# A masked attention and graph convolution kernel: the adjacency and the mask allocated ahead of the small constants

## The chip, the cores and the metric

The kernel runs on one core of one Trainium2 chip. The metric is device time in microseconds (us) of one execution; less is better. TensorE is called PE, its weight loads PEld, VectorE DVE, ScalarE ACT, GpSimd POOL, and SyncE SP.

## The reference

Two layers are applied to `x` of 32 batches x 512 nodes x 512 features, with one 512 x 512 adjacency of zeros and ones for all batches. The first is attention with 8 heads of 64 features, in which only neighbours count. The second is a graph convolution with the adjacency normalized by degrees. Each adds its input and ends in a layer norm.

```python
# layer 0
q, k, v = (x @ W + b, as 8 heads of 64)        # Wq, Wk, Wv: 512 x 512
scores = einsum('bihd,bjhd->bhij', q, k) / sqrt(64)
scores = scores + where(adj == 0, -1e9, 0)
x = layernorm(x + einsum('bhij,bjhd->bihd', softmax(scores), v))
# layer 1
d = rsqrt(adj.sum(axis=1))                     # 0 where the degree is 0
norm_adj = adj * d[:, None] * d[None, :]
x = layernorm(x + einsum('nm,bmo->bno', norm_adj, x @ weight) + bias)
```

## The kernel before

All the work is in `unshifted` (line 50). `general` (line 1006) is a fallback for numbers out of range, which a test at the end starts only where it is needed.

**Memory.** Tiles come from pools. `consts` (line 87) holds what lives through the whole kernel; its tiles lie one behind the other in the order in which the program asks for them, each rounded up to 32 bytes per partition. `acts`, `work` and `small` lie behind it. A tile of 128 partitions has the same offset in each of them. The pool `consts` begins with the large tiles `xT`, `wv`, `wk`, `wq`, `w1` and the bias rows; then, from line 240 on, come `ident`, `minus_half`, `half`, `sel`, `spread`, `FINE`, and then `maskT`, `adjT` and `dis`. `FINE` takes 160 bytes, two and a half times 64. In the built program `maskT` begins at byte 93,856 and `adjT` at byte 95,904 of each partition; both leave 32 when divided by 64. All other large tiles leave 0.

**What the two tiles hold.** `adjacency(m)` (line 264) transposes a block of 128 columns of the adjacency on PE, and makes two tiles of it: `maskT`, one byte per element (255 where there is no edge), and `adjT`, the transposed adjacency, 4 blocks of 512 elements of 4 bytes in the type fp32r. All other matmul operands but the two that go with it are plain fp32. This happens once, in the first batch.

**Who reads them.** `scores` (line 402) reads `maskT` on DVE: one instruction of 1024 elements for each pair of heads and block of keys, which takes the scores out of PSUM and subtracts the mask; ACT then takes the exponential. `convolve` (line 666) reads `adjT` as the moving operand of its matmuls. The degree scaling is in the other operand: `norm` and `low` write the scaled input as two fp32r tiles, `HI` (its rounded value) and `LO` (what is left), and `first(d)` adds up both products:

```python
for m in range(NT):
    tensor.matmul(p, HI[b][:, m, ts(d, P)], adjT[:, m, :], start=m == 0, stop=False)
    tensor.matmul(p, LO[b][m][:, ts(d, P)], adjT[:, m, :], start=False, stop=m == NT - 1)
take(d, p, scalar.copy)
```

With 4 values of d, 4 of m and 2 parts that makes 32 matmuls of 128 x 128 weights on 128 x 512 moving elements in each of the first 31 batches. The last batch runs the same 32 in another order, in `block(m)`, as soon as each part is there. `compare(m)` reads `adjT` on DVE four times in the first batch.

**The other matmuls.** All 512 x 512 products with weights (`keys_and_queries`, `values_of`, and `second` in `convolve`) go through `seven` or a like list of 7 pieces in the place of 8 (sums and differences of halves of the operands are made beforehand on DVE and POOL). Each piece is of matmuls with 256 moving columns into one PSUM bank. `scores` and `values` are the attention's two products, with 512 moving columns and 64 rows or columns of the array each.

**The order.** Every engine's instructions stay in the order in which the program issues them (`InOrder`, line 34), and this order is written out by hand in the loop over blocks of one batch and two heads (from line 864). A batch's convolution stands among the attention of the next one, as a list of pieces. After `first` come the combinations of zT on POOL (`parts`), the rest of a set of keys and queries for the batch after on PE, and then `second`. Of PSUM's eight banks, three pairs (`WIDE`, line 95) go round among scores and pieces, one more bank takes every fourth piece, and one holds the product with the values.

Of the kernel before, what the change touches and what calls it, by code (L numbers as in the profile page):

```python
# [11 lines left out]
U8 = mybir.dt.uint8  # L12
F32R = mybir.dt.float32r
# [4 lines left out]
P = 128  # L18
# [31 lines left out]
def unshifted(  # L50
# [29 lines left out]
    B, N, D = x.shape  # L80
    NT = N // P
# [5 lines left out]
    consts = ctx.enter_context(tc.tile_pool(name="consts", bufs=1))  # L87
# [27 lines left out]
    def load_x(b, j):  # L115


        if b == 1 and j == 1:
            X[b, j] = work.tile([P, 8, DT, 32], F32, name="x1", tag="e", bufs=6)
        else:  # L120
            X[b, j] = acts.tile([P, 8, DT, 32], F32, name="x", bufs=1)
        for q in range(4):
            nc.sync.dma_start(
                X[b, j][32 * q : 32 * (q + 1)],
                x[b, ts(j, HALF), ts(q, P)].rearrange("(k s) (t r) -> s k t r", s=32, r=32),
            )
# [109 lines left out]
    if B > 1:  # L236
        load_x(1, 0)
        load_x(1, 1)

    ident = consts.tile([P, P], F32, name="ident")  # L240
    make_identity(nc, ident)
    minus_half = consts.tile([P, NT], F32, name="minus_half")
# [12 lines left out]


    FINE = consts.tile([P, B + 2 * NT], F32, name="fine")
    maskT = consts.tile([P, NT, N], U8, name="maskT")
    adjT = consts.tile([P, NT, N], F32R, name="adjT")
    dis = consts.tile([P, NT], F32, name="dis")  # L260

    plainT = acts.tile([P, NT, N], F32, name="plainT", tag="hi", bufs=1)
# [977 lines left out]
def kernel(tc: tile.TileContext, *args: bass.AP):  # L1240


    bad = unshifted(tc, *args)
    with tc.If(bad > 0):
        general(tc, *args)
# [39 lines left out]
```

## Time and profile before

| | us |
|---|---|
| median of three runs | 2773.66 (2773.32 to 2774.48) |
| span of the profiled execution, first to last instruction | 2771.4 |
| PE busy | 2748.6 |
| DVE busy | 2237.2 |
| POOL busy | 1786.7 |
| ACT busy | 1053.9 |
| matmuls with adjT and HI, 496 in 31 batches | 201.7 |
| matmuls with adjT and LO, 496 in 31 batches | 196.0 |

The profile is of one execution, and its page gives that execution's span and no other time of its own; the median of the runs is 2.3 us above the span. Nearly every line of the page says L44, the line of the helper through which all instructions pass, so a group is known by its tiles: `mm<-adjT,hi` is a matmul into a bank `mm` that reads `adjT` and `hi`. Of a matmul the page gives the latency. Matmuls are pipelined, so what one takes of PE's time is the distance from its start to the start of the next, which the timeline gives. A plain fp32 matmul stands in the trace as two records, and one with fp32r operands as one.

### The profile page before, as it was taken

To read this page: it belongs to the slowest core of one execution; us is meant where nothing else is said; L and a number is where in the kernel's file an instruction comes from. 1 tells how busy PE (TensorE), PEld (TensorE's weight loads), DVE (VectorE), ACT (ScalarE), POOL (GpSimd) and SP (SyncE) were. 2 spreads that over 40 slices of the span, in tenths; PEclk is the share of its full clock that TensorE was granted. 3 is DMA by queue.
4 is the path that set the end of the run, shared out by engine and by line. 5 is a ranking of instruction groups with operands and counts; after the bars stand their busy time and mean duration, and the time that the engine had idled before them with its cause. 6 is when DMAs were issued, how large, how long until landed. Compare 5 with 4: busy or idle time off the path is not lost. (4 is left out here: it accounts for less than half of the span.)

```text
span 2771.4 us, 34559 instructions
## 1 busy us (share of the span) xinstructions
PE 2748.6 (99%) x12540; PEld 1882.6 (68%) x12540; DVE 2237.2 (81%) x3199; ACT 1053.9 (38%) x1324; POOL 1786.7 (64%) x1171
## 2 busy tenths in 40 slices
PE   9999999999999999999999999999999999999997
PEld 7667676676776766766767667676676676766755
DVE  6878888778877788878887878887778887888787
ACT  2234333434334343343433343433434334343343
POOL 3666567666676666766666766667666676666666
PEclk9999999999999999999999999999999999999999
DMA  4111112111121111211112211112111121111211
GB/s 122 35 39 40 51 55 51 50 45 46 54 61 43 51 45 48 60 46 54 39 51 56 49 52 46 46 54 62 43 50 46 47 60 46 54 39 51 64 35 51
DMA packets 379108, 141.05 MB, mean 51 GB/s; under 512 B 277808, under 2 KB 345392, under 8 KB 378928
## 3 DMA queue, kind: packets, MB, share of 16 engines
q1 hardware_dynamic: 377776, 137.17, 19.2%
q8 instruction: 101, 1.65, 0.3%
q10 hardware_dynamic: 1152, 1.57, 0.2%
q14 instruction: 79, 0.65, 0.1%
HBM read 71.83 MB, written 33.55 MB: 38 GB/s over the span
## 5 line engine op out<-in xcount | busy, mean ns | idle before, releaser
L44 ACT ACTIVATE e<-e 128x1024 f32<-128x1024 f32 x512 | 540.8, 1057 | 718.9 <-DVE e L44 699.9
L44 DVE SCALAR_TENSOR_TENSOR e<-sc,maskT 128x1024 f32<-128x1024 f32 x512 | 605.3, 1214 | 62.9 <-PE av L44 42.1
L44 POOL TENSOR_TENSOR acc<-acc,e 128x1024 f32<-128x1024 f32 x248 | 589.1, 2375 | 89.7 <-ACT e L44 77.5
L44 POOL TENSOR_TENSOR acc<-e 128x1024 f32<-128x1024 f32 x126 | 298.8, 2372 | 331.6 <-ACT e L44 331.4
L44 PE MATMUL sc<-kq 64*128 64x512 f32 x2048 | 476.7, 603 | 0.4 <-DVE e L44 0.4
L44 PE MATMUL av<-e,v 128*64 128x512 f32 x2048 | 467.9, 598 | 0.0
L44 PE MATMUL mm<-xT,wk 128*128 128x256 f32 x1792 | 463.3, 381 | 0.0
L44 PE MATMUL mm<-xT,wq 128*128 128x256 f32 x1792 | 459.9, 379 | 0.0
L44 PE MATMUL mm<-wv,xT 128*128 128x256 f32 x1792 | 401.4, 381 | 1.7 <-issue 1.2
L44 PEld LDWEIGHTS mm<-xT,wk 128*128 128x128 f32 x1792 | 337.3, 190 | 72.3 <-DVE e L44 26.0
L44 PEld LDWEIGHTS mm<-wv,xT 128*128 128x128 f32 x1792 | 335.4, 190 | 72.3 <-DVE e L44 24.3
L44 PEld LDWEIGHTS mm<-xT,wq 128*128 128x128 f32 x1792 | 340.5, 190 | 46.3
L44 PEld LDWEIGHTS sc<-kq 64*128 64x128 f32 x2048 | 183.6, 186 | 258.3 <-DVE e L44 118.3
L44 PEld LDWEIGHTS av<-e,v 128*64 128x64 f32 x2048 | 135.4, 136 | 316.3 <-issue 269.9
L44 POOL TENSOR_TENSOR yT<-yT,xr 128x512 f32<-128x512 f32 x124 | 153.7, 1270 | 149.2 <-DVE yT L44 149.2
L44 POOL TENSOR_TENSOR yT<-yT,b_r 128x512 f32<-128x512 f32 x124 | 157.3, 1304 | 140.2 <-DVE lo L44 140.2
L44 PE MATMUL mm<-w,zT 128*128 128x256 f32 x992 | 224.6, 379 | 0.0
L44 DVE TENSOR_TENSOR e<-e,mm 128x512 f32<-128x512 f32 x224 | 152.9, 683 | 82.9 <-PE mm L44 82.7
L44 ACT ACTIVATE y<-y,add,rstd 128x512 f32<-128x512 f32 x127 | 96.2, 805 | 317.3 <-POOL add L44 317.3
L44 PEld LDWEIGHTS mm<-w,zT 128*128 128x128 f32 x992 | 188.2, 190 | 27.0 <-DVE wq L44 0.8
L44 PE MATMUL mm<-adjT,hi 128*128 128x512 f32 x496 | 201.7, 407 | 0.0
L44 PE MATMUL mm<-adjT,lo 128*128 128x512 f32 x496 | 196.0, 395 | 0.0
(144 smaller groups left out, 3211.9 us busy)
## 6 DMA issues: line engine op xcount, KB each, us to landing
out_dram<-y SPq DMA_DIRECT2D x127, 256.0 KB, 2.1
x<-in_x_dram SPq DMA_DIRECT2D x248, 128.0 KB, 2.7
yT<-yb SPq DMA_DIRECT2D x496, 64.0 KB, 2.4
xr<-in_x_dram SPq DMA_DIRECT2D x122, 256.0 KB, 3.4
wk<-in_L_gnn_Wk_dram SPq DMA_DIRECT2D x8, 128.0 KB, 4.9
wq<-in_L_gnn_Wq_dram SPq DMA_DIRECT2D x8, 128.0 KB, 4.4
yT<-in_adj_dram SPq DMA_DIRECT2D x1, 1024.0 KB, 5.9
w<-in_L_gnn_weight_dram SPq DMA_DIRECT2D x2, 512.0 KB, 7.4
```

The lines of the kernel that those rows point to most:

```text
L44: return self.tc.keep_in_program_order(op(*args, **kwargs))
```

## The change

The two tiles are asked for before the small constants and no longer after them, with `adjT` first. Nothing else in the program is changed.

```diff
         load_x(1, 0)
         load_x(1, 1)
 
+    adjT = consts.tile([P, NT, N], F32R, name="adjT")
+    maskT = consts.tile([P, NT, N], U8, name="maskT")
     ident = consts.tile([P, P], F32, name="ident")
     make_identity(nc, ident)
     minus_half = consts.tile([P, NT], F32, name="minus_half")
...
     FINE = consts.tile([P, B + 2 * NT], F32, name="fine")
-    maskT = consts.tile([P, NT, N], U8, name="maskT")
-    adjT = consts.tile([P, NT, N], F32R, name="adjT")
     dis = consts.tile([P, NT], F32, name="dis")
```

In the built program `adjT` then begins at byte 92,352 and `maskT` at byte 100,544 of each partition, both multiples of 64. The six small tiles move up by 10,240 bytes, which is 160 times 64. `dis` and everything behind it keep their places, and each engine has the same instructions in the same order.

## The prediction

> **What bounds the kernel now.** I read the page's first two parts first, to see which engine sets the end.
>
> ```profile
> PE 2748.6 (99%) x12540; PEld 1882.6 (68%) x12540; DVE 2237.2 (81%) x3199; ACT 1053.9 (38%) x1324; POOL 1786.7 (64%) x1171
> ...
> PEclk9999999999999999999999999999999999999999
> ```
>
> TensorE is busy in 99% of the span at the full granted clock. A busy PE could still be a waiting PE, so the view of waits, limited to PE, comes second:
>
> ```profile
> PE mm L44 <- DMA xr<-in_x_dram: 4.6, 1, 4.6
> PE sc L44 <- DVE lo L44: 1.5, 1, 1.5
> PE mm L44 <- issue: 1.2, 1, 1.2
> ```
>
> These are its three longest; all of them together come to under 10 us in 2771 (the rest of PE's idle time lies before its first and behind its last matmul). PE waits for nobody in the loop, so what a matmul costs is what the kernel costs. Which matmuls cost more than they must? The third view is the list of groups with shapes kept apart (the last two numbers before the second bar are busy us and mean ns of one):
>
> ```profile
> L44 PE MATMUL mm<-xT,wq 128*128 128x256 f32 x1792 | 459.9, 379 | 0.0
> ...
> L44 PE MATMUL mm<-w,zT 128*128 128x256 f32 x992 | 224.6, 379 | 0.0
> ...
> L44 PE MATMUL mm<-adjT,hi 128*128 128x512 f32 x496 | 201.7, 407 | 0.0
> L44 PE MATMUL mm<-adjT,lo 128*128 128x512 f32 x496 | 196.0, 395 | 0.0
> ```
>
> A mean here is a latency, since matmuls overlap; the cost on PE is the distance from start to start. The timeline of PE in one batch gives it (start, length, then the instruction):
>
> ```profile
> 1030.16 0.59 PE L44 MATMUL mm<-adjT,hi 128*128 128x512 f32 x1
> 1030.59 0.40 PE L44 MATMUL mm<-adjT,lo 128*128 128x512 f32 x1
> 1030.82 0.39 PE L44 MATMUL mm<-adjT,hi 128*128 128x512 f32 x1
> 1031.05 0.40 PE L44 MATMUL mm<-adjT,lo 128*128 128x512 f32 x1
> ...
> 1037.59 0.39 PE L44 MATMUL mm<-adjT,lo 128*128 128x512 f32 x1
> 1037.82 1.03 PE L44 MATMUL mm<-xT,wk 128*128 128x256 f32 x4
> 1038.68 1.03 PE L44 MATMUL mm<-xT,wq 128*128 128x256 f32 x4
> 1039.55 1.03 PE L44 MATMUL mm<-xT,wk 128*128 128x256 f32 x4
> 1040.41 1.03 PE L44 MATMUL mm<-xT,wq 128*128 128x256 f32 x4
> 1041.27 1.03 PE L44 MATMUL mm<-w,zT 128*128 128x256 f32 x4
> ```
>
> From 1030.59 to 1037.82 stand 31 matmuls of adjT: 7.23 / 31 = 233.2 ns each. From 1037.82 to 1041.27 stand 16 records of plain fp32: 3.45 / 16 = 215.6 ns each. The same difference, 395 - 379 = 16 ns, is in the two mean latencies above.
>
> **How the two kinds compare.** keys_and_queries issues 2 x 7 x 2 x 2 = 56 matmuls a batch, 1792 in 32 batches; the page has 1792 records with wk and 1792 with wq, so a plain fp32 matmul is two records. convolve's first() issues 32 a batch, 992 in 31 batches, and the page has 496 + 496: an adjT matmul is one record. Two records for 256 fp32 columns take 431 ns, one record for 512 fp32r columns takes 233 ns. So per column a record of adjT takes 233.2 / 512 = 0.46 ns, and one of plain fp32 215.6 / 256 = 0.84 ns: the adjacency is streamed 1.85 times as fast as any other of the large moving operands. If reading the moving operand can ever be short, it is here.
>
> **What the Trainium skill says.** (1) "TensorE: Matmul & The Clock Gate", section "Back-to-back issue gap", gives N/2.4 + 2.5 ns between starts with a warm clock, 215.8 ns for N = 512. The 216 ns of the fp32 records agree if each is two passes of 256; adjT's 233 is 17.4 above it. (2) "FP8 and Floating Point Precision", "TensorE Precision Notes": true fp32 takes four passes, the reduced form reads 4-byte values and truncates them. Two records of two passes each, against one record, agree. (3) "SBUF — State Buffer", "A bandwidth-pool intuition that's wrong (but worth ruling out)", puts the moving operand's path at about 614 GB/s. adjT's matmuls read 128 x 2048 bytes in 233.2 ns, 1124 GB/s, so the trace disagrees with that as a ceiling and the measurement decides. (4) The same page's "Operand start alignment" is about what is legal, "not speed". So no page prices a start at 32 modulo 64; the estimate has to come from the trace.
>
> **The change part by part.** The instruction streams of the two programs are the same on all five engines; only addresses move. In the built program adjT begins at byte 95,904 of a partition (32 modulo 64) and goes to 92,352 (0 modulo 64). maskT goes from 93,856 (32) to 100,544 (0). ident, minus_half, half, sel, spread and FINE move up by 10,240 bytes, 160 x 64, and keep their remainder. dis and all that follows stay where they were. All other large moving operands (xT, wv, w1, kq, e, zT, parts) are at 0 modulo 64 already.
>
> - adjT as moving operand: the one item with a price. The trace shows no fp32r matmul with an aligned start, so I bound it. Best: the 215.8 ns that an array bound by its columns needs, 17.4 ns less than now. Zero: the 17.4 ns belong to streaming 4-byte elements at this rate, wherever they start. A loss isn't excluded (third rival). I take the best, because the excess appears exactly in the only operand that is both misaligned and streamed at the full rate. Its size hardly depends on the slice m, the output block or hi against lo (231 to 235 ns at most positions), which is what a property of the whole tile gives.
> - Sum: 31 batches x 32 x 17.4 ns = 17.3 us. The first matmul of a batch takes 430 ns rather than 233, on top of the columns, and should keep that extra. In the last batch the first 16 of the 32 matmuls stand among waits for lo and hi (2733.9 to 2739.8); the last 16 are back to back, 16 x 17.4 = 0.3 us. Together 17.6 us.
> - maskT: read by 512 DVE instructions of 1214 ns on 1024 elements, some 1.19 ns per element, the same as the transposes of 1236 that read no mask. Cost nothing either way; and DVE, at 81%, would hide it.
> - adjT's writes (four ACT casts of 586 ns, beside four ACT copies to plainT, already at 0 modulo 64, of 592 ns) and the four compares on DVE: nothing.
> - The moved small constants: same instructions, same remainders, nothing.
>
> **Does it reach the end?** A batch's adjT block would end 32 x 17.4 = 0.56 us sooner. What is late next is POOL's chain of zT differences, which second() needs:
>
> ```profile
> 1040.27 1.28 POOL L44 TENSOR_TENSOR parts<-zT 128x512 f32<-128x512 f32 x1
> 1041.63 1.27 POOL L44 TENSOR_TENSOR parts<-zT,parts 128x512 f32<-128x512 f32 x1
> ```
>
> POOL works on other things right before it, so it would not start sooner. The second result is there at 1042.90; PE takes it up at 1044.72, after two pieces that don't need it. That cover is 1.8 us, and 1.3 us are left with PE 0.56 sooner. DVE waits 1.6 us for PE's next piece at 1039.75, so it has room too, and being in step with PE in every batch neither debt adds up. I let all of it through: span 2771.4 - 17.6 = 2753.8. The page gives the profiled execution no time but its span; the median of the runs, 2773.66, lies 2.3 us above it, and I carry that over: 2756.1 us, 0.63% less.
>
> **Rivals.**
> 1. Nothing happens: the 17.4 ns are the price of streaming fp32r. For it: no other operand goes at this rate, so speed and alignment can't be told apart in this trace. Against it: the excess isn't a neat share of the 512 columns (8%). 2773.7 us.
> 2. Part of it: the read goes in pieces of 64 bytes, 33 of them with a start at 32 and 32 without, and the rate is short all the same. An estimate from the trace: (233.2 - 2.5) / 33 = 7.0 ns a piece, one piece less on 1008 matmuls: 7.1 us, 2766.6 us. A gain half eaten by a late POOL or DVE would end in the same region.
> 3. Slower: the weights of the next matmul (hi, lo, both at 0 modulo 64) are loaded during the running one. With adjT in the same phase their reads could hold each other up. At one 64-byte piece of adjT, 7.2 ns, for each of the 8 pieces of a 512-byte weight row, 58 ns on 1008 matmuls: +58 us, 2832 us. It decides from one such collision a matmul (over 5.5 ns, 5.6 us) if nothing is gained. Against it: plain fp32 loads weights under aligned operands with no trace of it, though at the lower rate.
>
> **How the numbers follow.** Full gain 0.65, part 0.12, nothing 0.15, slower 0.08. A measurement of this kernel can tell about 0.2%, 5.5 us, from no change; the part case (7.1 us) is beyond that. So faster 0.77, same 0.15, slower 0.08. The full gain alone reaches from 2753 (the 2.5 ns go as well, 1008 x 2.5 = 2.5 us) to 2759. With part it holds 0.77, too little, so the range reaches to no change: 2753 to 2775.
>
> **What would show it.** Right: the 31 adjT matmuls from the second on in 6.69 us rather than 7.23, latencies near 379, every other PE distance as before, PE's waits still under 10 us. Rival 1: 233 again. Rival 2: some 226. Rival 3: over 235, or longer weight loads than 188 ns. Wrong in the last step: 216 ns but new PE waits for POOL parts or DVE.

## The result and the profile after

The changed kernel takes 2769.49 us (median of 21 runs, 2768.87 to 2771.20) against 2773.55 us before (21 runs). The ratio is 0.9986, with a 95% interval of 0.9980 to 0.9993: faster, by 4.1 us or 0.15%. The forecast was a gain of 17.6 us. The span of the profiled execution went from 2771.4 to 2767.6 us.

The page's first part and the groups of matmuls, after:

```profile
PE 2744.6 (99%) x12540; PEld 1882.7 (68%) x12540; DVE 2238.2 (81%) x3199; ACT 1053.5 (38%) x1324; POOL 1786.1 (65%) x1171
...
L44 PE MATMUL mm<-xT,wq 128*128 128x256 f32 x1792 | 459.9, 379 | 0.0
...
L44 PE MATMUL mm<-w,zT 128*128 128x256 f32 x992 | 224.6, 379 | 0.0
...
L44 PE MATMUL mm<-adjT,hi 128*128 128x512 f32 x496 | 200.0, 403 | 0.0
L44 PE MATMUL mm<-adjT,lo 128*128 128x512 f32 x496 | 194.4, 392 | 0.0
```

Of the groups shown only the two of adjT have moved, by 4 and 3 ns of latency. The same place of PE's timeline (start, length, instruction) gives the distances:

```profile
1028.98 0.58 PE L44 MATMUL mm<-adjT,hi 128*128 128x512 f32 x1
1029.40 0.40 PE L44 MATMUL mm<-adjT,lo 128*128 128x512 f32 x1
...
1036.28 0.39 PE L44 MATMUL mm<-adjT,lo 128*128 128x512 f32 x1
1036.51 1.02 PE L44 MATMUL mm<-xT,wk 128*128 128x256 f32 x4
```

From 1029.40 to 1036.51 stand 31 matmuls, 229.4 ns each, against 233.2 before and the 215.8 that were forecast. In what follows a distance is the mean over the last three quarters of the block (its last matmul left out) in 28 batches: 233.3 ns before and 229.0 ns after, 4.4 ns less before rounding. Times 1008 matmuls they are 4.4 us; over whole blocks the two means are 233.4 and 229.4 ns, which makes 4.0 us. Both agree with the measured 4.1 us, within its noise. PE's waits are as short as before:

```profile
PE mm L44 <- DMA xr<-in_x_dram: 4.7, 1, 4.7
PE sc L44 <- DVE lo L44: 1.5, 1, 1.5
PE mm L44 <- issue: 1.3, 1, 1.3
```

So the gain came from the expected place and went through to the end in full. Three quarters of the forecast are missing, and they are missing in the matmul itself; the question of the experiments is what the other 13 ns of each are.

Three theories were set against each other. Reading: the moving operand comes out of memory at a limited rate, which depends on where it starts. Fixed cost: every fp32r matmul, or every weight load beside one, pays something whatever its length. Type: the fp32r element or single-pass matmul is slower by itself.

### The profile page after: what moved, and what is told of

Read it like the earlier page. It is cut to its first block, busy times and chain, and to the rows that moved or that the text cites. A ratio compares the mean times of both kernels' runs of the same rounds, so it can differ in the third digit from the quotient of the medians.

```text
span 2767.6 us, 34559 instructions
## 1 busy us (share of the span) xinstructions
PE 2744.6 (99%) x12540; PEld 1882.7 (68%) x12540; DVE 2238.2 (81%) x3199; ACT 1053.5 (38%) x1324; POOL 1786.1 (65%) x1171
## 4 chain that ended last, share of the span: by engine, by line
PE 96%; DVE 2%; POOL 1%; issue 0%; ACT 0%; DMA 0%; POOLq 0%; DVEq 0%
PE mm L44 64%; PE sc L44 17%; PE av L44 16%; POOL acc L44 0%; DVE st L44 0%; POOL xT L44 0%; DVE e L44 0%; DVE wv L44 0%; DMA xr<-in_x_dram 0%; DVE u L44 0%; DVE mv L44 0%; DVE y L44 0%; POOL yT L44 0%; DVE yT L44 0%; DVE xT L44 0%
```

## Experiments

All start from the changed kernel. Ratios are to the kernel before, which was run beside each of them, with 95% intervals. Its median lay between 2773.3 and 2774.1 us in the four sets of runs, so a difference of under 1 us between the times of two experiments says nothing; there the distances decide.

**Where adjT starts.** Five kernels give adjT some room and move it inside by k elements (what lies behind it moves on by the 128 bytes of the room):

```diff
-    adjT = consts.tile([P, NT, N], F32R, name="adjT")
+    adjT_room = consts.tile([P, NT * N + 32], F32R, name="adjT")
+    adjT = adjT_room[:, k : k + NT * N].rearrange("p (m n) -> p m n", m=NT)
```

k = 8 elements, 32 bytes, the remainder of the kernel before, with the mask still in its new place:

> The changed kernel with adjT alone moved on by 32 bytes, so that it begins at 32 modulo 64 again, while maskT stays at 0 modulo 64. If adjT's start alone made the gain, the adjT matmuls stand 233.2 ns apart again and the time is that of the kernel before, 2773.5 us. If the mask had a part in it, the time stays below 2772 us. If a moved neighbour did it all, the distance stays at 229 ns and the time at 2769.5 us.

Measured: 233.4 ns, 2773.1 us, ratio 0.9999 (0.9990 to 1.0007).

```profile
1030.27 0.39 PE L44 MATMUL mm<-adjT,lo 128*128 128x512 f32 x1
...
1037.50 1.02 PE L44 MATMUL mm<-xT,wk 128*128 128x256 f32 x4
```

The 31 matmuls between take 7.23 us, 233.2 ns each, as before the change. So adjT's start alone made the gain; of the mask and the moved constants no effect can be seen.

k = 1, 4 bytes:

> adjT begins at 4 modulo 64. Theory A (the moving operand is read in pieces of 64 bytes, and a start inside a piece costs one piece more, 33 and not 32): 233 ns and 2773.5 us, as with 32. Theory B (a finer grain of 16 or 32 bytes counts too, and a start that breaks it costs more): over 234 ns and over 2774.5 us. Theory C (only a start in the second half of a 64-byte piece costs): 229 ns, 2769.5 us.

Measured: 238.5 ns, 2779.18 us, ratio 1.0019 (1.0012 to 1.0027). Theory B: a finer grain than 64 bytes counts too. Latencies in the view of tile adjT (minimum, median, maximum in ns) show the step, first of the changed kernel, then of this one:

```profile
L44 PE MATMUL mm<-adjT,hi x496: 388/392/586, 177.1 to 2703.4; 128*128 128x512 f32 x166
L44 PE MATMUL mm<-adjT,lo x496: 387/392/496, 177.6 to 2703.7; 128*128 128x512 f32 x166
```

```profile
L44 PE MATMUL mm<-adjT,hi x496: 394/403/589, 177.2 to 2712.5; 128*128 128x512 f32 x166
L44 PE MATMUL mm<-adjT,lo x496: 394/403/493, 177.7 to 2712.8; 128*128 128x512 f32 x166
```

The median goes from 392 to 403 ns, though adjT has only moved by 4 bytes and what lies behind it by 128.

k = 4, 16 bytes:

> adjT begins at 16 modulo 64. The starts so far gave 226.9 ns (0 modulo 256), 229.0 (64 modulo 128), 233.4 (32 modulo 64) and 238.5 (4 modulo 64). If a broken unit of 16 bytes is what made 4 worse than 32, 16 costs as much as 32: 233 ns, 2773.5 us. If the unit is 32 bytes, 16 is as bad as 4: 239 ns, 2779 us.

Measured: 234.6 ns, 2774.43 us, ratio 1.0004 (0.9994 to 1.0014). It is near 32 bytes, 1.2 ns above it, and not near 4; a broken unit of 16 bytes is the better description.

k = 16, 64 bytes, which makes adjT start at 0 modulo 256:

> adjT begins at 0 modulo 256 rather than at 64 modulo 128. Theory A (64 bytes are the grain): nothing changes, 229 ns and 2769.5 us. If pieces are larger than 64 bytes and the changed kernel still begins inside one, the 13 ns that are left above 215.8 go, in part or in full: down to 216 ns and 2756 us.

Measured: 226.9 ns, 2768.31 us, ratio 0.9981 (0.9973 to 0.9988). In the same place of the timeline:

```profile
1028.03 0.39 PE L44 MATMUL mm<-adjT,lo 128*128 128x512 f32 x1
...
1035.06 1.03 PE L44 MATMUL mm<-xT,wk 128*128 128x256 f32 x4
```

That is 7.03 us, 226.8 ns each. The changed kernel's start, 64 modulo 128, was not the best one, but the 13 ns did not go either: 2.1 ns went.

k = 48, with 64 elements of room (256 bytes), which makes adjT start at 128 modulo 256:

> adjT begins at 128 modulo 256 (64 modulo 128 gave 229.0 ns, 0 modulo 256 gave 226.9). If 128 bytes are the grain, this is as good as 0 modulo 256: 226.9 ns, 2768.3 us. If 256 bytes are, it stands at 228 to 229 ns, 2769.5 us.

Measured: 226.8 ns, 2768.36 us, ratio 0.9980 (0.9972 to 0.9988). So 128 bytes are as good as 256. With these starts the distance goes from 226.8 to 238.5 ns, and at its best it is still 11 ns above 215.8.

**Fixed cost or share of the columns.** Each matmul in two of 256 columns:

```diff
-            for m in range(NT):
-                tensor.matmul(p, HI[b][:, m, ts(d, P)], adjT[:, m, :], start=m == 0, stop=False)
-                tensor.matmul(p, LO[b][m][:, ts(d, P)], adjT[:, m, :], start=False, stop=m == NT - 1)
+            for n in range(2):
+                at = slice(n * HALF, (n + 1) * HALF)
+                for m in range(NT):
+                    tensor.matmul(p[:, at], HI[b][:, m, ts(d, P)], adjT[:, m, at], start=m == 0, stop=False)
+                    tensor.matmul(p[:, at], LO[b][m][:, ts(d, P)], adjT[:, m, at], start=False, stop=m == NT - 1)
```

> first() does each matmul of 512 columns as two of 256 (the second half of the columns after the eight of the first), so 64 adjT matmuls a batch of half the length, with as many more weight loads; what is computed is the same. If what is left above 215.8 ns is a share of the columns (a rate of reading): 115 to 116 ns a matmul, a batch's block longer by 0.1 us, 2772 us. If it is a fixed cost of every fp32r matmul, or of every weight load beside one: 106.7 + 2.5 + 13 = 122 ns, a block longer by 0.5 us, 2785 us.

Measured: 115.1 ns, 2771.98 us, ratio 0.9994 (0.9985 to 1.0003). Two halves take 230.2 ns, 1.2 more than one whole. But this mean hides two levels: 17 of the 31 batches stood at 113.3 ns and 14 at 117.8, each of them steadily. One batch of either kind:

```profile
944.93 0.28 PE L44 MATMUL mm<-adjT,lo 128*128 128x256 f32 x1
...
952.35 1.03 PE L44 MATMUL mm<-xT,wk 128*128 128x256 f32 x4
```

```profile
1030.31 0.28 PE L44 MATMUL mm<-adjT,lo 128*128 128x256 f32 x1
...
1037.45 1.02 PE L44 MATMUL mm<-xT,wk 128*128 128x256 f32 x4
```

63 matmuls take 7.42 us in the first and 7.14 us in the second. The forecast for a fixed cost of 13 ns per matmul or per weight load was 122 ns, and both levels are below it, so that is out; on the mean, the excess goes with the columns. What chooses the level is not shown. adjT, `hi` and `lo` have one place each in these batches, so a start alone doesn't fix the distance: two matmuls take 226.7 ns at the lower level, as much as one at the best start, and 235.6 at the upper.

**Weights.** Half as many columns of weights (`take` gets the rows to copy as an argument, which isn't shown):

```diff
-                tensor.matmul(p, HI[b][:, m, ts(d, P)], adjT[:, m, :], start=m == 0, stop=False)
-                tensor.matmul(p, LO[b][m][:, ts(d, P)], adjT[:, m, :], start=False, stop=m == NT - 1)
-            take(d, p, scalar.copy)
+                at = slice(d * P, d * P + 64)
+                tensor.matmul(p[:64], HI[b][:, m, at], adjT[:, m, :], start=m == 0, stop=False)
+                tensor.matmul(p[:64], LO[b][m][:, at], adjT[:, m, :], start=False, stop=m == NT - 1)
+            for at in (0, 64):
+                take(d, p[:64], scalar.copy, slice(at, at + 64))
```

> The adjT matmuls of first() load only 64 columns of weights in the place of 128 (it leaves out half of the output features, and copies the other half twice). Moving reads as in the changed kernel. If the weight loads of the next matmul hold the stream up, half of the 13 ns goes: 222 ns. If the stream is alone responsible: 229 ns. The time itself also has 128 more copies on ACT, which has room.

Measured: 228.3 ns, 2769.29 us, ratio 0.9985 (0.9978 to 0.9993). The loads got shorter (134 ns rather than 188), the distance by only 0.7 ns. And the weights' own start, 32 bytes on:

```diff
-                    HI[b], LO[b] = (acts.tile([P, NT, D], F32R, name=k, bufs=1) for k in ("hi", "lo"))
+                    HI[b], LO[b] = (
+                        acts.tile([P, NT * D + 16], F32R, name=k, bufs=1)[:, 8 : 8 + NT * D].rearrange(
+                            "p (n d) -> p n d", n=NT
+                        )
+                        for k in ("hi", "lo")
+                    )
```

> HI and LO, the weights of the adjT matmuls, begin at 32 modulo 64 in the first 31 batches; adjT stays as in the changed kernel. If only the moving operand's start counts: 229 ns, 2769.5 us. If both reads are in each other's way by their phase: 231 ns or more, or 227 or less.

Measured: 230.0 ns, 2771.38 us, ratio 0.9992 (0.9983 to 1.0001). That is 1.0 ns more for the weights' start alone, little beside the 13 ns. By the distance it would be 1 us; the medians are 1.9 us apart.

**Two bytes rather than four.** The type of the three tiles:

```diff
-F32R = mybir.dt.float32r
+F32R = mybir.dt.bfloat16
```

> The changed kernel with adjT, HI and LO in bfloat16 rather than fp32r: 2 bytes per element and the same 992 matmuls of 512 columns (it changes the computation: what LO keeps is rounded to bfloat16). If what is left above 215.8 ns is a limit on reading 4-byte elements: 216 ns, a block of 7.1 us and 2756 us. If it is of the array, of PSUM, or of single-pass matmuls: 229 ns as before, 2769.5 us.

Measured: 215.9 ns, 2756.27 us, ratio 0.9939 (0.9916 to 0.9961).

```profile
1024.13 0.38 PE L44 MATMUL mm<-adjT,lo 128*128 128x512 bf16 x1
...
1030.82 1.03 PE L44 MATMUL mm<-xT,wk 128*128 128x256 f32 x4
```

The 31 matmuls take 6.69 us, 215.8 ns each. The whole excess is gone, so it isn't a price of the array, of PSUM or of every single-pass matmul of 512 columns. But this edit changes the type, the element and the memory read at once, and of the weights too. Two ways of reading the same fp32r elements from other places came first:

```diff
+                again = adjT[:, m, None, :16].to_broadcast([P, 32, 16])
+                q = p.rearrange("p (k n) -> p k n", n=16)
-                tensor.matmul(p, HI[b][:, m, ts(d, P)], adjT[:, m, :], start=m == 0, stop=False)
-                tensor.matmul(p, LO[b][m][:, ts(d, P)], adjT[:, m, :], start=False, stop=m == NT - 1)
+                tensor.matmul(q, HI[b][:, m, ts(d, P)], again, start=m == 0, stop=False)
+                tensor.matmul(q, LO[b][m][:, ts(d, P)], again, start=False, stop=m == NT - 1)
```

> Each adjT matmul streams the first 16 columns of its block 32 times over, in the place of 512 different columns (it leaves out the other columns of the adjacency). Same number of elements, type and weights, but only one piece of 64 bytes is ever read. If the cost is in going on to the next piece of memory: 216 ns, 2756 us. If it is in handing over 4-byte elements at this rate, or in starting every piece: 227 to 229 ns, 2768 to 2770 us.

Measured: 242.7 ns, 2781.07 us, ratio 1.0024 (1.0012 to 1.0036). Neither expectation: it is slower than any start. The order of reading may matter, so a run with the pieces out of order asks whether the break or the same address did it; only the two patterns differ from the edit above:

```diff
-                again = adjT[:, m, None, :16].to_broadcast([P, 32, 16])
-                q = p.rearrange("p (k n) -> p k n", n=16)
+                there = adjT[:, m].rearrange("p (k two n) -> p two k n", two=2, n=16)
+                q = p.rearrange("p (k two n) -> p two k n", two=2, n=16)
```

> Each adjT matmul reads its 512 columns in another order, first the even and then the odd runs of 16 columns (64 bytes each), and writes them to their own places in PSUM, so what is computed is the same. If the 243 ns of the run that read one piece over and over came from breaking the run after every 64 bytes: 243 ns, 2782 us. If they came from the same address again: 229 ns, 2769.5 us.

Measured: 240.0 ns, 2780.49 us, ratio 1.0022 (1.0013 to 1.0031). Breaking the run every 64 bytes costs 11 ns of distance without reading an address twice, most of what same_piece lost. This edit writes PSUM in the broken order too, and the run doesn't part the two; but same_piece writes its columns in order and takes even longer, so the way in which the moving operand is read does cost by itself.

**Memory gone over, or element.** The last two kernels part what bfloat16 had changed together. First bfloat16 elements with 4 bytes of room each, over the type of the run above:

```diff
-    adjT = consts.tile([P, NT, N], F32R, name="adjT")
+    adjT_wide = consts.tile([P, NT, N, 2], F32R, name="adjT")
+    adjT = adjT_wide[:, :, :, 0]
```

> adjT, HI and LO in bfloat16, as before, but each element of adjT has 4 bytes of room, so that a row of 512 lies over the same 2048 bytes as the fp32r one, and begins at the same place (it changes the computation as the other bfloat16 run does). If the 13 ns above 215.8 are the price of going over 2048 bytes of memory in the time of 512 columns, whatever is taken from them: 229 ns, 2769.5 us. If they belong to handing over 4-byte elements or to the type: 216 ns, 2756 us.

Measured: 226.7 ns, 2766.99 us, ratio 0.9975 (0.9965 to 0.9985). This is neither of the two forecasts, 229 and 216, but close to the first. Then fp32r elements, each used twice:

```diff
+                twice = adjT[:, m, :HALF, None].to_broadcast([P, HALF, 2])
+                q = p.rearrange("p (n k) -> p n k", k=2)
-                tensor.matmul(p, HI[b][:, m, ts(d, P)], adjT[:, m, :], start=m == 0, stop=False)
-                tensor.matmul(p, LO[b][m][:, ts(d, P)], adjT[:, m, :], start=False, stop=m == NT - 1)
+                tensor.matmul(q, HI[b][:, m, ts(d, P)], twice, start=m == 0, stop=False)
+                tensor.matmul(q, LO[b][m][:, ts(d, P)], twice, start=False, stop=m == NT - 1)
```

> Each adjT matmul of 512 columns reads the first 256 elements of its row, every one twice running (it leaves out the second half of the adjacency's columns). Type and number of elements are as in the changed kernel, the memory gone over is half. If going over memory is the price: 222 ns or less, 2763 us or less. If the fp32r element is the price: 229 ns, 2769.5 us. If what counts is how long the contiguous runs are, as with the scattered and repeated pieces: over 240 ns.

Measured: 215.8 ns, 2756.87 us, ratio 0.9942 (0.9919 to 0.9964). The timelines of PE show both; first bf16_wide:

```profile
1028.47 0.39 PE L44 MATMUL mm<-adjT,lo 128*128 128x512 bf16 x1
...
1035.26 0.39 PE L44 MATMUL mm<-adjT,lo 128*128 128x512 bf16 x1
1035.49 1.02 PE L44 MATMUL mm<-xT,wk 128*128 128x256 f32 x4
```

Then each_twice:

```profile
1025.11 0.38 PE L44 MATMUL mm<-adjT,lo 128*128 128x512 f32 x1
...
1031.58 0.38 PE L44 MATMUL mm<-adjT,lo 128*128 128x512 f32 x1
1031.80 1.03 PE L44 MATMUL mm<-xT,wk 128*128 128x256 f32 x4
```

31 matmuls take 7.02 us in the first (226.5 ns each) and 6.69 us in the second (215.8). bf16_wide differs from bf16_adj only in the room of adjT's elements. Two-byte elements spread over 2048 bytes cost what fp32r costs at its best start, and fp32r elements out of 1024 bytes cost nothing extra. So the type is out. bf16_wide alone could also mean a price for every step over a gap; each_twice, which has no gaps and loses the excess by going over less memory, speaks against it. Together the two say that the 11 ns are for going over 2048 bytes in the time of 512 columns.

**Does the start matter to slower streams?** bf16_adj with adjT 4 bytes on, and w1, plain fp32, 4 bytes on:

```diff
+    adjT_room = consts.tile([P, NT * N + 32], F32R, name="adjT")
+    adjT = adjT_room[:, 2 : 2 + NT * N].rearrange("p (m n) -> p m n", m=NT)
-    adjT = consts.tile([P, NT, N], F32R, name="adjT")
...
+    w1_room = consts.tile([P, 14 * HALF + 16], F32, name="w1")
+    w1 = w1_room[:, 1 : 1 + 14 * HALF].rearrange("p (i u o) -> p i u o", i=7, u=2)
-    w1 = consts.tile([P, 7, 2, HALF], F32, name="w1")
```

> Two misaligned moving operands that need less per time: adjT, HI and LO in bfloat16 (as in the run before, with the same rounding of LO) with adjT 4 bytes past a multiple of 64, and w1, plain fp32, 4 bytes past a multiple of 64 as well. If a start costs only where 4-byte elements are streamed at the full rate: 215.9 ns for adjT and 215.6 to 216 for the matmuls of w with zT and parts, 2756 us. If every start inside a piece costs: adjT at 220 ns or more and w at 220 or more, 2762 us or more.

Measured: adjT 216.6 ns and w with zT 216.8 (216.1 before, both means over whole blocks), 2759.07 us, ratio 0.9947 (0.9927 to 0.9967). A start 4 bytes off costs 0.7 ns here, where the fp32r stream paid 11.7 (238.5 - 226.8).

## Why the prediction was wrong

**What bounds the kernel, and that it reaches the end: right.** In most runs the time follows the distance to within 1 us. bf16_adj stands 13.1 ns below the changed kernel, times 1008 that is 13.2 us, and 13.2 us were measured; start_4 stands 9.5 ns above, 9.6 us, and 9.7 were measured. The widest miss is same_piece, 13.6 us by the distance and 11.6 measured. The cover on POOL and DVE held too: in bf16_adj PE's longest waits are 4.6 us for a DMA and 1.7 for `lo`, as short as before. Where bf16_adj took away the full 17.4 ns of the prediction's sum, it reached 2756.27 us, 0.2 from the number forecast for the alignment alone.

**What moves and what doesn't: right.** The mask and the small constants cost nothing that could be seen, as start_32 shows; ACT's casts into adjT took 586 ns before and 585 after. A detail was misread: the first matmul of a block doesn't take 430 ns of PE. The four records ahead of it start at 1029.49 and need 4 x 215.6 ns, which is up to 1030.35; its own record starts at 1030.16, so 0.19 us of it lie ahead of its turn. No number hung on it.

**The price of the start: wrong, and it is the step that failed.** "I take the best, because the excess appears exactly in the only operand that is both misaligned and streamed at the full rate." Both marks were on the same tile, and the text gave the whole 17.4 ns to the first one. The term was mis-sized: it measured 4.4 ns, and 6.5 at the best start; 11 ns belong to the second mark, the rate. Rival 1 had said as much: "no other operand goes at this rate, so speed and alignment can't be told apart in this trace". That sentence leaves open any share between the two, but a share for each was given only 0.12. That 2769.49 us lies between 2753 and 2775 is no merit of the argument: the range was drawn out to no change, and the full gain would have ended by 2759.

**The rivals.** Rival 2 came nearest: both causes at once. Its size was too large: one of 33 pieces would have been 7.1 us, against 4.1. Its count is not the rule either, since a start at 4 bytes costs 5.1 ns more than one at 32, which 33 pieces each don't explain. Rival 1 named the larger share. Rival 3's loss didn't come, but it has a trace of truth: 1.0 ns when the weights' start moves, and in start_4 weight loads of 192 ns rather than 188. Whether a start costs by itself, or by the way in which the two reads fall together, no run has parted.

**The distance that was aimed at.** The 215.8 ns for 512 columns by the formula in the Trainium skill's "TensorE: Matmul & The Clock Gate", "Back-to-back issue gap", hold here for bfloat16 (215.9) and for fp32r out of 1024 bytes (215.8). They don't hold for fp32r out of 2048 bytes (226.8 at best), and the prediction used them there though, as it says itself, the trace shows no fp32r matmul with an aligned start. The section itself gives the formula for an isolated matmul and about 131 ns for a stream of weight loads and matmuls; no adjT matmul of 512 columns came below 215.8 here, so the measurement speaks for the formula.

**Open.** Which part of the path between memory and PE sets the limit, and why the steps by start are what they are (226.8, 229.0, 233.4, 234.6 and 238.5 ns for 128, 64, 32, 16 and 4 bytes), isn't settled by these runs. The two levels of halves at one start say that it isn't the start of the stream alone. Only these starts were tried, of fp32r rows of 512.

**Better than both kernels.** With the same computation, start_256 and start_128 are some 1.1 us below the changed kernel by their medians. Their intervals overlap with its own; the distances, 2.1 ns shorter, are what shows it. With adjT, HI and LO in bfloat16, and the coarser LO that this means, it is 2756.27 us.

## What to carry to other kernels

When one operand differs from all others in two ways, the trace can't say which of them costs: give each a share, or keep the whole range open, and separate them by a run that changes one. Count what a matmul reads per column and not only its columns: a single-pass stream of 4 bytes per column stood 5% above the distance of its columns at the best start and 10% at the worst, and there the start of the tile is worth a look. In this kernel the fp32r operand did best at a multiple of 128 bytes; for bfloat16 and plain fp32 a start 4 bytes off cost 0.3%. And look at single batches before trusting a mean: the one of halves agreed with its forecast, and no batch stood at it.

## What was not expected

- Reading 64-byte runs out of order costs 11 ns a matmul (240.0 against 229.0), and one run over and over costs 14 (242.7), though the second touches 64 bytes of a partition in all.
- The best start gives 2048 / 226.8 = 9.0 bytes per ns and partition; 512 columns of 4 bytes at 215.8 would be 9.5. The Trainium skill's "SBUF — State Buffer", "A bandwidth-pool intuition that's wrong (but worth ruling out)", puts the path of the moving operand at about 614 GB/s for bf16. bf16_adj agrees, with 128 x 1024 bytes in 215.9 ns, 607 GB/s; but the fp32r stream reads 128 x 2048 bytes in 226.8 ns, 1156 GB/s, so in bytes that figure is no ceiling.
- The grain goes up to 128 bytes: 64 modulo 128 costs 2.1 ns more than 0 modulo 128. With bfloat16 elements in 4 bytes of room and the start at 64 modulo 128 this step wasn't seen (226.7).
